# Scaling the rows of the later groups' scans three slots ahead of their step, and not two

## The chip, the cores and the metric

The kernel runs on one core of one Trainium2 chip. The metric is the time of the kernel on the device in microseconds. The median of three runs of the kernel before is 3759.6 us (3755.57 to 3771.47).

## What is computed

The input x has 32 sequences of 256 tokens with 256 features. The result is `x + ffn(cond(x))`, all in fp32. Cut to what matters here:

```python
def cond(x, t_emb, ...):
    xr, gate = split(x @ W_in.T, 2)            # 512 inner features each
    xc = silu(causal_conv(xr + t_emb, 4 taps))
    xn = layernorm(xc)
    B, C, dt = split(xn @ W_xproj.T, 3)        # 16 states each
    ad = 1 - 0.01 * tanh(dt @ W_dt.T + b_dt) * tanh(A_log)
    bd = B * min(norm(xn), 1)
    for t in range(256):                       # the scan
        h = clip(h * ad[t] + bd[t] * xn[t], -10, 10)   # h: 32 x 16 x 512
        y[t] = sum over the 16 states of C[t] * h
    return (y + D * xn) * silu(gate) @ W_out.T

def ffn(x):                                    # two layers
    x = x + local_attention(shift(x))          # 8 heads of 64, window 128
    x = x + (a * gelu(g)) @ w2                 # a, g from layernorm(shift(x)) @ w1
```

The scan is serial in its 256 tokens. Attention and feed-forward of a sequence need the scan's output for that sequence, and nothing of other sequences.

## The kernel before

**Tiling of the scan.** The 32 sequences are cut into four groups (NG) of eight (GB). For a group the state h is one tile of 128 partitions (16 states of 8 sequences) by 512 inner features. The 256 steps of a group are cut into eight chunks of 32 (CH). The kernel divides the state by the running product of the decays, so that the decay leaves the loop: within a step there remains `h = clamp(h + xrep, +-lim)`, where xrep is the token's row of xn, times a factor beta for each partition. Four functions carry one step:

- `load_rows` (L672): SyncE (SP) issues a DMA that reads the token's row of xn from DRAM and spreads it over the 128 partitions. It moves 256 KB into a tile of the pool xp, which has six buffers (L225). The tile is called xrep.
- `scale_row` (L689 to L698): ScalarE (ACT) multiplies the tile by beta, in place (the instruction is that of L693).
- `step` (L700 to L707): VectorE (DVE) makes the new h with one custom instruction (L703). The pool hp has eight buffers of h. With it the xrep buffer comes free, so the load of row n+6 can start when step n has ended.
- `read_out` (L710 to L721): four 32-column matmuls on TensorE (PE) multiply four states h by C. They free the buffers of h.

**What a chunk needs beforehand.** The input is projected (L395) and convolved: `conv_in` on GpSimd (acc, L474), `conv_taps` on VectorE (acc, L485), `conv_th` on ScalarE (th, L493), `conv_out` on VectorE (xc, L498). Then it is normalised (st, mv, ve, stat, xn; L547 to L566) and written to DRAM as xnd. Out of it come the chunk's figures: `figures_in` (bcd, L614), `decay_th` (ad, a tanh on ScalarE, L628) and `decays` (L633 to L647), in which VectorE finishes beta (L641). No row of the chunk can be scaled before that.

**Order by slots.** The work of a scan is put into slots. `at(s, function, ...)` puts a call into slot s, and in the slot of step t of a chunk that starts at s0 the calls are: the step of row t; the load of row t+6; the scale of row t+2. Beta is due in slot s0-5, and `read_out` of four rows five slots after the first of them. Each slot has two parts: the agenda with the step is traced first, the one with loads and scales after it.

**Order by stages.** Group 0's scan runs alone (`alone` is true for it), and a part of its rows is spread by TensorE and not by a DMA (`by_tensor`). Afterwards the scan of the next group runs beside attention and feed-forward of the group before it. These are cut into stages, eight for each sequence and layer, 128 for each group. After each stage `scan_to` advances the scans by a number of slots, two on average (L1466 on). So the calls of both are traced interleaved. After the third group's attention no scan is left, and the last group's attention and feed-forward run by themselves.

**What the builder does.** Out of the traced calls the builder makes each engine's queue of instructions. It takes the traced order as priority, but puts an instruction further ahead or behind by when it reckons it to be ready. A few calls are held, among them the scales of the later groups: `tc.keep_in_program_order(scaled)` (L698) keeps each behind what was traced before it on ScalarE. Scales of different rows may still change places: rows 0, 2, 4, 14 and 30 of a chunk are scaled three to five rows ahead of an earlier row in nearly every chunk.

**Attention and feed-forward** beside it, with the names that the trace uses: ps_qkv (L962), the matmuls of the projection to q, k and v; sq (ACT, L975), rot, swp and ss (DVE and POOL, L978 to L995), which normalise and rotate q and k; qT and kT (ACT, L1006), which take the turned q and k out of PSUM; sc, pT and v_sb (L1143 to L1177), the scores and their exponentials; oT (ACT, L1213; DVE, L1230), the attention's output; rinv (DVE, L1195); hn and hT, the normalised input of the feed-forward; pa (PE, L1301) and ag (ACT, L1309; DVE, L1317), its widening matmuls and the gated product; po_f and fo (L1329, L1340), the narrowing. All matmul results share one tag of PSUM with eight banks (L229).

Of the kernel before, what the change touches and what calls it, by code (L numbers as in the profile page):

```python
# [73 lines left out]
def kernel(  # L74
# [139 lines left out]
    for i in range(2):  # L214
        t = const.tile([P, NI * (P + GB)], FP, tag=f"ly{i}", name=f"ly{i}")
# [3 lines left out]
    def program(ctx, exact):  # L219
# [153 lines left out]
        def group_scan(g):  # L373
# [8 lines left out]
            alone = g == 0  # L382
# [5 lines left out]
            def at(s, what, *args):  # L388
                agendas[-1].setdefault(s, []).append(partial(what, *args))
# [276 lines left out]
            def by_tensor(t):  # L666
                return alone and t % (2 * NQ) < XR
# [171 lines left out]
            for c in range(NCH):  # L839
                s0 = c * CH  # L840
# [35 lines left out]
            for c in range(NCH):  # L876
                s0 = c * CH
                at(s0 - 43 if alone else s0 + 6, load_x, c)
                if alone:
                    for ch in range(NC_):  # L880
                        at(s0 - 40 + 2 * ch, project, c, ch)
                else:
                    for i in range(2):
                        at(s0 - 44 + 2 * i, load_projected, c, i)
                for ch, s in enumerate((13, 16, 17, 18)):
                    at(s0 + s, project, c, NC_ + ch)
                at(s0 - 27, raw_sums, c)
                for j in range(NJ):
                    at(s0 - 26 + 4 * j, norm_turn, c, j)
                at(s0 - 8, figures_out, c)  # L890
                for t in range(CH):
                    if not by_tensor(t):
                        at(s0 + t - 6, load_rows, c, t)
                    if by_tensor(t) and t % XR == 0:
                        at(s0 + t - 4, spread_rows, c, t)
                    at(s0 + t - 2, scale_row, c, t)
                for hb in range(CH // TB):
                    s = s0 + hb * TB
                    at(s - 9 if alone else s + 7, load_skip, c, hb)
                    at(s + 23, out_turn, c)  # L900
                for d in range(KM):
                    at(s0 + 43 + 2 * d, project_y, c, d)
# [11 lines left out]
        def scan_slots(groups):  # L914


            slots, scans = {}, [group_scan(g) for g in groups]
            for part in range(2):
                for i, agendas in enumerate(scans):
                    for s, what in agendas[part].items():  # L920
                        slots.setdefault(i * S + s, []).extend(what)
            for s in range(min(slots), max(slots) + 1):
                for what in slots.get(s, ()):
                    what()
                yield s
# [531 lines left out]
        s0 = done[0]  # L1457
# [130 lines left out]
```

## Time and profile before

| | |
|---|---|
| median of three runs | 3759.6 us |
| the profiled execution's own time | 3750.83 us |
| its span, first to last instruction | 3748.7 us, granted clock 0.987 |
| group 0's scan alone | 0 to about 460 us |
| scans of groups 1 to 3 beside attention and feed-forward | about 460 to 2910 us |
| last group's attention and feed-forward alone | 2910 to 3749 us |
| one chunk of 32 steps in the joint phase | about 108 us, 3.4 us for each slot |
| step (DVE L703) | 1024 instructions, 926 ns on average |
| scale (ACT L693) | 960 instructions, 719 ns on average |
| load of a row (256 KB) | 960, 3.3 to 4.0 us from issue to landing |

The profile is one execution. A group of instructions is given by line, engine, operation and tiles (out<-in), then its count, its busy time in us, the mean of one in ns, and the engine's idle time just before such instructions with what ended most of it. In the timeline each line has its start in us, its duration in us, the engine and the line, and in square brackets the idle time before it and what released it. In a list of waits the three numbers are the sum of the waits in us, their number and the longest. In the table of stretches each pair is an engine's busy time and its number of instructions, in the order PE, PEld (weight loads), DVE, ACT, POOL, and after them the granted clock, the share of the DMA engines and GB/s.

### The profile page before, as it was taken

How to read it: one execution, taken by the hardware profiler on the slowest of the kernel's cores; microseconds unless marked ns; L12 is line 12 of the kernel's file. 1: busy time of each engine (PE TensorE's matmuls, PEld its weight loads, DVE VectorE, ACT ScalarE, POOL GpSimd, SP SyncE). 2: the span in 40 equal slices, each digit the busy share in tenths (PEclk: the TensorE clock that was granted, in tenths of full speed). 3: DMA queues.
4: the chain of work that ended last, by engine and by line, in shares of the span. 5: the costliest groups of instructions: out<-in, count | busy, mean ns of one | idle time of the engine just before them, and what ended most of it. 6: DMA issues, size and time to landing. Idle time of an engine off the chain costs nothing.

```text
span 3748.7 us, 57254 instructions
## 1 busy us (share of the span) xinstructions
PE 3601.1 (96%) x19900; PEld 2242.4 (60%) x19900; DVE 2669.6 (71%) x5177; ACT 2195.4 (59%) x3817; POOL 1834.9 (49%) x1776
## 2 busy tenths in 40 slices
PE   7999889999999999999999999999999999999998
PEld 4444335656656665665666665656666666666666
DVE  6888889888787787778777877777777444444443
ACT  4666656666666666666666665666666444444442
POOL 4433466545555565455455555645444444434441
PEclk9999999999999999999999999999999999999999
DMA  7777655445454545434444545444443211011101
GB/s 210 205 198 202 189 163 149 120 117 135 127 137 129 147 123 146 120 112 122 120 128 116 147 124 147 121 108 126 112 129 103 57 40 50 12 34 34 30 25 35
DMA packets 469214, 435.81 MB, mean 116 GB/s; under 512 B 228835, under 2 KB 308532, under 8 KB 468788
## 3 DMA queue, kind: packets, MB, share of 16 engines
q1 hardware_dynamic: 384466, 420.05, 40.1%
q10 hardware_dynamic: 84450, 12.01, 2.0%
q8 instruction: 160, 2.62, 0.3%
q14 instruction: 138, 1.13, 0.1%
HBM read 383.70 MB, written 46.66 MB: 115 GB/s over the span
## 4 chain that ended last, share of the span: by engine, by line
PE 62%; DVE 16%; POOL 7%; ACT 6%; DMA 5%; issue 3%; SPq 0%; ACTq 0%; DVEq 0%; POOLq 0%
PE ps_qkv L962 12%; PE pa L1301 12%; PE po_f L1329 7%; DVE h L703 6%; PE y L715 4%; PE ps_wo L1012 4%; DMA xrep<-xnd 4%; PE sc L1168 4%; PE ov L1206 3%; PE ps_out L793 2%; ACT xrep L693 2%; DVE acc L485 2%; PE tr_qk L1001 2%; PE ps_in L395 2%; POOL acc L474 2%
## 5 line engine op out<-in xcount | busy, mean ns | idle before, releaser
L703 DVE CUSTOM_DVE_ANT_0 h<-h,xrep,lim 128x512 f32<-128x512 f32 x1024 | 948.2, 926 | 269.2 <-ACT xrep L693 238.8
L693 ACT ACTIVATE xrep<-xrep,beta 128x512 f32<-128x512 f32 x960 | 674.1, 719 | 333.0 <-DMA xrep<-xnd 235.9
L962 PE MATMUL ps_qkv<-qkv,res 128*128 128x512 f32 x1536 | 727.1, 610 | 45.2 <-DVE ag L1317 30.1
L1301 PE MATMUL pa<-hT,w 128*128 128x256 f32 (+1 forms) x3072 | 688.3, 386 | 0.3 <-ACT oT L1213 0.3
L1301 PEld LDWEIGHTS pa<-hT,w 128*128 128x128 f32 (+1 forms) x3072 | 492.9, 178 | 183.7 <-issue 66.5
L962 PEld LDWEIGHTS ps_qkv<-qkv,res 128*128 128x128 f32 x1536 | 282.4, 194 | 335.4 <-issue 263.3
L986 POOL TENSOR_TENSOR rot<-rot,swp 128x512 f32<-128x512 f32 x256 | 336.5, 1314 | 293.0 <-DVE swp L983 239.2
L1258 POOL TENSOR_TENSOR rstd<-ve,neg_half 128x1 f32<-128x1 f32 x128 | 82.7, 646 | 792.9 <-DVE ve L1256 787.8
L994 POOL TENSOR_TENSOR rn<-ss,neg_half 128x8 f32<-128x8 f32 x256 | 460.3, 1798 | 14.8 <-DVE ss L992 5.0
L1329 PE MATMUL po_f<-ag,w 128*128 128x256 f32 (+1 forms) x1536 | 387.8, 394 | 4.8 <-DVE res L1340 1.1
L715 PE MATMUL y<-h,ly 128*32 128x512 f32 x2048 | 354.9, 612 | 12.9 <-DVE h L703 11.7
L1329 PEld LDWEIGHTS po_f<-ag,w 128*128 128x128 f32 (+1 forms) x1536 | 273.6, 190 | 112.9 <-issue 44.6
L1317 DVE SCALAR_TENSOR_TENSOR ag<-pa,b_sb,ag 128x256 f32<-128x256 f32 (+1 forms) x448 | 212.4, 474 | 166.5 <-ACT ag L1309 163.0
L975 ACT ACTIVATE sq<-ps_qkv 128x512 f32<-128x512 f32 x256 | 152.1, 596 | 270.5 <-PE ps_qkv L962 234.6
L995 POOL TENSOR_TENSOR rot<-rot,rn 128x512 f32<-128x512 f32 x256 | 298.6, 1166 | 20.1
L1309 ACT ACTIVATE ag<-pa,b_sb 128x256 f32<-128x256 f32 x320 | 150.4, 470 | 198.5 <-PE pa L1301 197.4
L1012 PE MATMUL ps_wo<-oT,wo 128*128 128x256 f32 x1024 | 231.6, 379 | 0.0
L485 DVE SCALAR_TENSOR_TENSOR acc<-xr,wc_sb,acc 128x256 f32<-128x256 f32 x384 | 192.7, 525 | 52.9 <-POOL acc L474 52.6
L1177 ACT ACTIVATE pT<-sc 128x512 f32<-128x512 f32 x384 | 208.5, 596 | 32.2 <-PE sc L1168 30.7
L1168 PE MATMUL sc<-qT,kT 64*128 64x128 f32 (+1 forms) x2048 | 221.5, 345 | 0.0
L978 DVE TENSOR_TENSOR rot<-ps_qkv,rc_sb 128x512 f32<-128x512 f32 x256 | 175.0, 683 | 56.5 <-ACT sq L975 55.9
L1012 PEld LDWEIGHTS ps_wo<-oT,wo 128*128 128x128 f32 x1024 | 194.5, 190 | 27.2 <-PE y L715 0.8
(150 smaller groups left out, 5534.7 us busy)
## 6 DMA issues: line engine op xcount, KB each, us to landing
xrep<-xnd SPq DMA_DIRECT2D x960, 256.0 KB
rb<-inv SPq DMA_DIRECT2D x128, 256.0 KB
xnd<-xn SPq DMA_DIRECT2D x64, 256.0 KB
qkv<-in_wqkv_dram SPq DMA_DIRECT2D x24, 512.0 KB
ahead<-xs_a SPq DMA_DIRECT2D x48, 256.0 KB
xp<-ahead SPq DMA_DIRECT2D x48, 256.0 KB
xd<-xnd SPq DMA_DIRECT2D x192, 64.0 KB
w<-in_w_dram SPq DMA_DIRECT2D x80, 128.0 KB
```

What stands on the lines that cost most here:

```text
L485: nc.vector.scalar_tensor_tensor(acc, xr[:, :, k : k + CH], wc_sb[:, ch, k : k + 1], acc, ALU.mult, ALU.add,)
L693: scaled = nc.scalar.activation(bx, ck[c].pop(("bx", t), bx), AF.Copy, scale=ck[c]["beta"][:, t : t + 1])
L703: nc.vector._custom_dve(TENSOR_ADD_SAT, out=h_new, in0=state["h"], in1=bx, s0=ck[c]["lim"][:, 0, t : t + 1], s1=ck[c]["lim"][:, 1, t : t + 1],
L715: nc.tensor.matmul(ck[c]["y", hb][32 * q : 32 * q + 32, :], ly[hb % 2][:, 32 * t : 32 * t + 32], ck[c].pop(("h", hb * TB + t)), start=(i = ...
L962: nc.tensor.matmul(ps, res[b][:, k, t0 : t0 + W], wt["qkv", a][:, k], start=(k == 0), stop=(k == KM - 1),)
L986: nc.gpsimd.tensor_add(rot, rot, swp)
L994: nc.gpsimd.tensor_tensor(rn, ss, neg_half, ALU.pow)
L995: nc.gpsimd.tensor_mul(rot, rot, bc(rn, 2, DH))
L1012: nc.tensor.matmul(po[:, d], wt["wo", 0][:, c, d * P : (d + 1) * P], oT[:, c, :], start=(c == 0), stop=(c == NC_ - 1),)
L1168: nc.tensor.matmul(banks[r][:, i, :], kT[rows, i0 + i, kw * W : (kw + 1) * W], qT[rows, i0 + i, kw * W :], start=False, stop=(i == n - 1),)
L1301: nc.tensor.matmul(pg if x else pa, wt["w1", m][:, k, x], self.h[:, k], start=(k == 0), stop=(k == KM - 1),)
L1329: nc.tensor.matmul(self.po[:, d], wt["w2", 0][r0 : r0 + n, m, d * P : (d + 1) * P], self.ag[m][r0 : r0 + n], start=(m == 0), stop=(m == le ...
```

## The change

One line of `group_scan` is changed. The scale of row t of a later group (`alone` is false) is put three slots ahead of step t, and not two. For group 0 it stays two slots. Load, step and read-out stay in their slots, and so do the buffers and what the functions do. In the slot of step t the scale that is called is now that of row t+3; its place behind the previous ACT instruction is held as before.

```diff
                     if not by_tensor(t):
                         at(s0 + t - 6, load_rows, c, t)
                     if by_tensor(t) and t % XR == 0:
                         at(s0 + t - 4, spread_rows, c, t)
-                    at(s0 + t - 2, scale_row, c, t)
+                    at(s0 + t - 2 if alone else s0 + t - 3, scale_row, c, t)
```

## The prediction

> **What bounds the kernel now.** I read the busy shares first, then the chain that ended last, the costliest groups, the busy time of three stretches, the waits of a steady stretch, and the timeline of one chunk.
>
> ```profile
> PE 3601.1 (96%) x19900; PEld 2242.4 (60%) x19900; DVE 2669.6 (71%) x5177; ACT 2195.4 (59%) x3817; POOL 1834.9 (49%) x1776
> ...
> PE 62%; DVE 16%; POOL 7%; ACT 6%; DMA 5%; issue 3%; SPq 0%; ACTq 0%; DVEq 0%; POOLq 0%
> ...
> L703 DVE CUSTOM_DVE_ANT_0 h<-h,xrep,lim 128x512 f32<-128x512 f32 x1024 | 948.2, 926 | 269.2 <-ACT xrep L693 238.8
> L693 ACT ACTIVATE xrep<-xrep,beta 128x512 f32<-128x512 f32 x960 | 674.1, 719 | 333.0 <-DMA xrep<-xnd 235.9
> ```
>
> TensorE is the bound: the scan can only cost time where it keeps TensorE waiting. Steps wait 238.8 us for scaled rows and scales wait 235.9 us for loads, which looks like the prize of an earlier scale; the next views show how little of it TensorE feels.
>
> ```profile
> 0.00:460.00 460.00, 407.20 (x1689) 207.54 (x1690) 376.12 (x719) 269.07 (x495) 186.12 (x266) 0.95 0.74 201
> 2000.00:2500.00 500.00, 480.94 (x2759) 302.80 (x2755) 386.90 (x746) 311.13 (x547) 268.13 (x257) 0.99 0.46 127
> 2910.00:3749.00 839.00, 827.89 (x4722) 559.31 (x4719) 362.82 (x783) 380.88 (x623) 333.96 (x278) 1.00 0.13 35
> ```
>
> The columns are the stretch in us, its length, and busy time of PE, PEld, DVE, ACT and POOL. In the first stretch group 0 scans alone, and in the last nothing scans; the change touches neither. Between lies the joint phase, some 2450 us. In its steady part TensorE is idle 500 − 480.94 = 19.1 us in 500. By its gaps it is idle 26.8 us in 430 to 645 and 59 us in 645 to 2700: no change of the scan's order can win more than these.
>
> ```profile
> DVE h L703 <- ACT xrep L693: 61.1, 32, 3.6
> ...
> PE ps_qkv L962 <- DVE ag L1317: 10.4, 5, 2.7
> ```
>
> These are waits between 2000 and 2500 (sum, number, longest). The steps wait 61.1 us; TensorE's one regular stall, 10.4 us in 5 waits, is about one per chunk of 32 steps. Over the joint phase there are 13 such stalls, from 1310.79 to 2606.19, 108 us apart, 30.1 us in sum. The timeline shows how one comes about:
>
> ```profile
> 2139.33 0.48 DVE L485 SCALAR_TENSOR_TENSOR acc<-xr,wc_sb,acc 128x256 f32<-128x256 f32 x1 [0.93 <-POOL acc L474]
> ...
> 2142.11 2.01 POOL L474 TENSOR_SCALAR acc<-xr,wc_sb,bconv_sb 128x256 f32<-128x256 f32 x1 [2.66 <-DVE xc L498]
> ...
> 2160.71 0.72 ACT L693 ACTIVATE xrep<-xrep,beta 128x512 f32<-128x512 f32 x1 [2.75 <-DVE beta L641]
> ...
> 2168.33 0.72 ACT L693 ACTIVATE xrep<-xrep,beta 128x512 f32<-128x512 f32 x1 [3.56 <-DMA xrep<-xnd]
> 2170.18 0.81 DVE L703 CUSTOM_DVE_ANT_0 h<-h,xrep,lim 128x512 f32<-128x512 f32 x1 [3.42 <-ACT xrep L693]
> ...
> 2172.75 4.31 PE L962 MATMUL ps_qkv<-qkv,res 128*128 128x512 f32 x6 [2.58 <-DVE ag L1317]
> ```
>
> At each chunk's start the first row's scale stands at the head of ACT's queue until VectorE has beta. Then a row scaled out of turn (804, five rows ahead) waits 3.56 us for its load, since that load was issued only when step 798 freed a buffer at 2164.70. Rows 799 and 800 queue behind it, VectorE waits 3.42 us, and the ag behind step 800 reaches TensorE 2.58 us late.
>
> **What the Trainium skill says.** "PSUM — Partial Sum Buffer", section "Engine vs sequencer instructions", has the queues of ScalarE, VectorE and GpSimd as strict FIFO. The trace agrees: behind the scale of 804 the copy of oT stands, its matmul done at 2162.6, and it starts at 2168.96. "SBUF — State Buffer", section "Who interferes with whom", says that a VectorE instruction with two SBUF inputs and a GpSimd instruction that reads SBUF exclude each other. A step has two such inputs, h and xrep: it takes 0.81 us in most places and 1.84 at 2157.97, beside GpSimd's products; the mean is 0.926. A step that moves can pay or save up to 1.0 us. "Perfetto Trace Analysis", section "Optimization Strategy", tells to find the engine's gaps and what blocks it; the 13 equal gaps are where I price the change.
>
> **The change, part by part.** It takes nothing away and adds nothing: 768 scales of 0.72 us on ACT are called one slot earlier, after a different ACT instruction, to which their order is then held. The rest is traced as before, but the builder orders each engine anew. I read the order of both programs as built, engine by engine, and set it against the times of the trace.
>
> ACT: 616 of the 768 scales move, by 3.4 instructions on average. Each place that held row t holds row t+1. The rows scaled far ahead of their turn remain: before, rows 0, 2, 4, 14 and 30 of a steady chunk go 3 to 5 rows ahead; after, rows 1, 3, 5, 15 and 31. So the waits for loads remain as well, shifted by a row: a row five ahead still needs the buffer of the step just before it (six buffers). Row 1 takes the place where row 0 waits for beta, and row 0's scale, which needs beta too, stands before it: the same wait. Cost of this part: nothing.
>
> SP: 250 of 768 row loads move two places up. A load leaves 0.03 us after the step six rows earlier has ended and lands 3.3 to 4.0 us later; its moment is set by the step and not by SP. Other loads on SP's queue lose at most that wait, and none of the 13 stalls ends on one. Nothing.
>
> VectorE: 511 of 768 steps move up, by 4.9 positions, mostly one step in the place of its forerunner. Rows 12 to 18 of a chunk stay, where the y matmuls, four rows at a time, must free h buffers (eight). TensorE: 131 of 11,553 instructions move, so its demand is the same. GpSimd: 330 of 1759, following.
>
> What is then different on the chain to the stall? In the chunk of the timeline two steps (792 and 793) come ahead of two xc instructions and an acc that waits 0.93 us for GpSimd. Their scales can end by 2139.2; the second step takes 0.81 after that and ends at 2140.05, and the second xc can begin near 2140.5 in place of 2141.52: 1.0 us earlier. GpSimd's acc, which waited 2.66 us for xc, starts 1.0 us earlier, and with it the acc and rot ahead of beta. One more acc (0.48) leaves this stretch and returns ahead of beta, net nothing; between rot and beta four steps stand before and after. So beta comes about 1.0 us earlier, the links after it are the same, and the stall of 2.58 shrinks to 1.6. Its bounds: 0, where the acc waits elsewhere; and 2.5 to 3.0, if the steps in between also meet less of GpSimd.
>
> Against it: in this chunk the tanh of conv (th) goes behind two scales and is 1.5 to 2.2 us later; the conv's xc for it is 2.4 us later (2137.65 to 2140.05), but GpSimd needs its result only 1.8 later, within its own 2.66 wait. That cover is part of the sum above; without it 0.6 us is lost.
>
> Rows 14 and 15 are the risky place. Before, the order is scale 810, a table load, ag, sq, xn, scales 813 and 814; after, scale 811, xn, scales 814 and 815, then table load and ag. Row 815's load needs step 809. The trace has step 808 from 2190.05 to 2190.86; if step 809 follows it directly, it ends at 2191.7, the row lands 3.5 later at 2195.2, the scale ends at 2195.9, the table load (1.28) at 2197.2. The ag ran at 2195.99, so it is 1.2 us late; but the sq behind it waited for TensorE until 2197.77, and the ag after it has until 2201.6. So nothing reaches TensorE.
>
> Sum: 13 steady chunks × 1.0 = 13 us less. The chunks of 460 to 1290 don't repeat, and I add nothing for them, ±10. Against the profiled execution (3750.83, span 3748.7 and 2.1 around it) that gives 3737.8; the median of the runs is 8.8 higher, 3759.6, and so 3746.6, say 3747.
>
> **The rivals.** *Full gain:* beta comes 2.5 to 3 us earlier and the 13 stalls go. For: the wait is one serial chain and each link is short. Against: the beta, load and scale links are unchanged in number. It gives −30 us (the 30.1 of the waits), 3730; with the small stalls beside them (0.8 for scores and 0.9 for rinv in every other chunk, 11 us) 3719. What is late next is then TensorE itself.
>
> *Nothing changes:* the one-row shift leaves every wait in its place, and the freed microsecond goes back to the next row's load. For: the out-of-turn rows are the same pattern. It gives 3760 ± 5. That the edit doesn't do what it says is ruled out by the 616 moved scales.
>
> *Slower:* ACT stands at its queue's head for a row that hasn't landed, with TensorE's evacuations behind it. Place: row 15 ahead of the table load and ag, and rows 1 to 5 likewise. With step 809 at its old end, 2192.69, the row lands at 2196.2, the scale ends at 2196.9 and the table load at 2198.2: ag is 2.2 us late and the sq behind it 0.9. Eight banks hold all matmul results, so once both are late, TensorE waits. It decides when step 9 of a chunk ends later than about 1 us after its new place. If two such places a chunk pass on 1.5 us each, 14 chunks give 42 us: 3802. For: 235.9 us of ACT's idle time are such waits already, and the steps of rows 12 to 18 don't move up with their scales. Against: only one of the pairs stands directly before an evacuation without slack.
>
> **How the numbers follow.** About 0.5% (18.8 us) is what a measurement of this kernel can tell from no change. Small gain 0.40 (3747, its own range 3736 to 3758), nothing 0.12, full gain 0.18, slower 0.30. Faster by over 0.5% is below 3740.8: the full gain less a little, and a fifth of the small gain, 0.17 + 0.07 = 0.24. Slower is above 3778.4: 0.28 of the 0.30. The same: 0.48. The range runs from the full gain's lower end, 3719, to the slower case's 3802, which leaves out about 0.15 above and 0.03 below.
>
> **What would show it.** Right: the 13 stalls of ps_qkv on ag near 1.6 us each, the sum of the waits 560 to 2910 near 17 and not 30.1; beta about 1 us nearer to rot; steps' wait for scales near 239 us; the stretch of 839 us after the last step unchanged. Wrong: new TensorE stalls on ag or sq near rows 14 to 16 of a chunk, with an ACT wait for xrep's load just ahead of them (the slower rival); no such stalls left at all (full gain); or a gain or loss in the chunks before 1290, for which my sum has no term.

## The result and the profile after

| | before | after |
|---|---|---|
| median | 3759.94 us (20 runs) | 3768.05 us (20 runs) |
| ratio, 95% interval | | 1.0024, 1.0014 to 1.0033 |
| span of the profiled execution, granted clock | 3748.7 us, 0.987 | 3763.8 us, 0.986 |

Three slots are 8 us slower. The forecast was 13 us faster: wrong in its sign, though both changes are within half a per cent. The two profiled executions differ by 15.1 us, of which 6.1 us are there already when group 0's last step starts (459.9 and 466.0 us), in a part that the change doesn't touch; so single stretches of two profiles are compared below, and the whole by the ratio.

The page of the kernel after, with the shares and the steps of the scan:

```profile
PE 3597.9 (96%) x19900; PEld 2240.2 (60%) x19900; DVE 2682.6 (71%) x5177; ACT 2196.7 (58%) x3817; POOL 1824.0 (48%) x1776
...
L703 DVE CUSTOM_DVE_ANT_0 h<-h,xrep,lim 128x512 f32<-128x512 f32 x1024 | 942.0, 920 | 192.3 <-ACT xrep L693 109.0
```

The work is the same and TensorE is the bound as before. VectorE's wait for scaled rows fell from 238.8 to 109.0 us, which is what an earlier scale is for, and the kernel is slower. The lists of waits from 560 to 2910 us, before and then after, show where VectorE waits instead: at ag, 91.9 us where it was 33.5, and at y's matmuls, for a free buffer of h, 21.0 where it was 4.2.

```profile
ACT xrep L693 <- DMA xrep<-xnd: 135.0, 66, 6.5
...
DVE ag L1317 <- ACT ag L1309: 33.5, 48, 2.5
...
DVE h L703 <- PE y L715: 4.2, 13, 1.9
```

```profile
ACT xrep L693 <- DMA xrep<-xnd: 154.2, 83, 5.7
...
DVE ag L1317 <- ACT ag L1309: 91.9, 63, 6.0
...
DVE h L703 <- PE y L715: 21.0, 13, 1.9
```

TensorE's idle time is the length of a stretch less the time in which TensorE is busy. The stretches run between the same qT copies in both traces:

| TensorE idle, us | before | after |
|---|---|---|
| first chunks (510 to 1352 us before) | 34.4 | 45.4 |
| steady chunks (1352 to 2647 us before) | 42.3 | 47.1 |

The runs below add traces with two and with three slots in a stretch, and the two kinds don't overlap: 34.2 to 38.5 us against 43.7 to 47.4 in the first chunks, 42.3 twice against 45.2 to 47.1 in the steady ones. But the table shows where TensorE waits, and not how much time is lost. The idle time rises by 15.8 us and the time by 8. The steady stretch even became shorter, 1295.6 us before and 1292.2 after, since TensorE was busy for 1253.3 us before and 1245.2 after, at a granted clock of 0.99 and 1.00. The first chunks became longer, 842.0 and 854.3 us.

TensorE's waits from 1310 to 2700 us, before and then after, show how the steady part changed:

```profile
PE ps_qkv L962 <- DVE ag L1317: 30.1, 13, 2.7
PE ps_qkv L962 <- DVE rinv L1195: 6.3, 12, 0.9
...
PE ov L1206 <- DVE ag L1317: 1.1, 6, 0.3
```

```profile
PE ps_qkv L962 <- DVE ag L1317: 19.8, 11, 2.4
PE ps_qkv L962 <- DVE rinv L1195: 11.4, 13, 0.9
PE ov L1206 <- DVE ag L1317: 10.0, 12, 1.1
PE tr_qk L1001 <- DVE ag L1317: 6.0, 7, 1.8
```

The stalls that the prediction priced fell by 10.3 us, and the gap at sc by 2.7 (from 4.9). Waits at ov, tr_qk and rinv rose by 8.9, 6.0 and 5.1.

**A steady chunk.** It is the chunk of the prediction's timeline. First TensorE's other gaps there before (the prediction shows the one of 2.58), then all of them after, then ScalarE after:

```profile
2147.61 0.38 PE L1161 MATMUL sc<-mask_t,ident_b 128*128 128x512 bf16 x1 [0.81 <-DVE ag L1317]
2161.07 1.52 PE L1206 MATMUL ov<-pT,v_sb 128*64 128x256 f32 x16 [0.15 <-DVE ag L1317]
2166.81 1.98 PE L962 MATMUL ps_qkv<-qkv,res 128*128 128x512 f32 x4 [0.21 <-DVE rinv L1195]
```

```profile
2163.92 0.38 PE L1161 MATMUL sc<-mask_t,ident_b 128*128 128x512 bf16 x1 [0.30 <-DVE ag L1317]
2178.35 1.52 PE L1206 MATMUL ov<-pT,v_sb 128*64 128x256 f32 x16 [1.11 <-DVE ag L1317]
2185.08 1.99 PE L962 MATMUL ps_qkv<-qkv,res 128*128 128x512 f32 x4 [0.94 <-DVE rinv L1195]
2190.01 2.41 PE L962 MATMUL ps_qkv<-qkv,res 128*128 128x512 f32 x5 [1.58 <-DVE ag L1317]
```

```profile
2177.99 0.72 ACT L693 ACTIVATE xrep<-xrep,beta 128x512 f32<-128x512 f32 x1 [3.85 <-DVE beta L641]
2178.61 0.57 ACT L1006 COPY qT<-tr_qk 128x512 f32<-128x512 f32 x1
```

The stall of 2.58 us at ps_qkv is 1.58, the size forecast. But ov, ahead of it, now waits 1.11 us and not 0.15 for an ag that stands behind beta on VectorE, and rinv costs 0.94 and not 0.21. (Before, rinv's wait was short in every other steady chunk; now it is 0.63 or more in all.) Before, the chunk had 0.81 + 0.15 + 0.21 + 2.58 = 3.75 us of gaps; now 0.30 + 1.11 + 0.94 + 1.58 = 3.93. From the start of that ov to ps_qkv it is 11.68 us before and 11.66 after: this part of the chain is no shorter, and the stall at its end is smaller only because TensorE comes to it later. VectorE shows why ov waits, before and then after:

```profile
2147.48 0.67 DVE L978 TENSOR_TENSOR rot<-ps_qkv,rc_sb 128x512 f32<-128x512 f32 x1
...
2160.54 0.48 DVE L1317 SCALAR_TENSOR_TENSOR ag<-pa,b_sb,ag 128x256 f32<-128x256 f32 x1
```

```profile
2163.78 0.68 DVE L978 TENSOR_TENSOR rot<-ps_qkv,rc_sb 128x512 f32<-128x512 f32 x1
...
2172.89 1.26 DVE L485 SCALAR_TENSOR_TENSOR acc<-xr,wc_sb,acc 128x256 f32<-128x256 f32 x1
2174.18 1.39 DVE L468 TENSOR_TENSOR xr<-xp,cond_sb 128x256 f32<-128x256 f32 x1
...
2177.82 0.48 DVE L1317 SCALAR_TENSOR_TENSOR ag<-pa,b_sb,ag 128x256 f32<-128x256 f32 x1
```

From rot to that ag it was 2147.48 to 2160.54, 13.06 us; now it is 2163.78 to 2177.82, 14.04. The acc that the steps displaced landed beside GpSimd's products (L995, L745), takes 1.26 us and not 0.48, and the xr behind it takes 1.39 and not 0.41. Before, a step and a small instruction stood there and took longer in the same way (1.84 for 0.81, 1.02 for 0.23). Set against the twelve matmuls of po_f that start at 2135.57 before and at 2152.37 after, GpSimd's acc (L474) comes 1.0 us earlier, as forecast, the ag ahead of rot 0.5 earlier, and beta 0.5 later.

**A first chunk.** ScalarE of the kernel after near 825 us:

```profile
827.24 0.72 ACT L693 ACTIVATE xrep<-xrep,beta 128x512 f32<-128x512 f32 x1 [2.25 <-DMA xrep<-xnd]
827.87 1.05 ACT L1213 COPY oT<-ov 128x512 f32<-128x512 f32 x2
```

Row 388 waits 4.53 us for its load, row 390 then the 2.25 shown, and both oT copies wait behind row 390. TensorE's waits from 560 to 1310 us, before (one line) and then after:

```profile
PE ps_qkv L962 <- ACT oT L1213: 1.8, 2, 1.3
```

```profile
PE ps_qkv L962 <- ACT oT L1213: 7.1, 3, 2.9
...
PE ov L1206 <- DVE res L1020: 4.8, 1, 4.8
...
PE ov L1206 <- DVE ag L1317: 3.5, 2, 2.2
```

Before, the wait of ov for res wasn't there. In the three waits for oT, ACT stands just ahead of the copy at rows 390, 479 and 513, whose loads haven't landed.

### The profile page after: what moved, and what is told of

It reads as the page before. It is cut to its first block, busy times and chain, and to the rows that moved or that the text cites. A ratio compares the mean times of both kernels' runs of the same rounds, so it can differ in the third digit from the quotient of the medians.

```text
span 3763.8 us, 57292 instructions
## 1 busy us (share of the span) xinstructions
PE 3597.9 (96%) x19900; PEld 2240.2 (60%) x19900; DVE 2682.6 (71%) x5177; ACT 2196.7 (58%) x3817; POOL 1824.0 (48%) x1776
## 4 chain that ended last, share of the span: by engine, by line
PE 65%; DVE 18%; DMA 6%; POOL 4%; issue 4%; ACT 3%; SPq 0%; ACTq 0%; DVEq 0%; POOLq 0%
PE ps_qkv L962 13%; PE pa L1301 12%; PE po_f L1329 8%; DVE h L703 6%; DMA xrep<-xnd 5%; PE y L715 4%; PE sc L1168 4%; PE ps_wo L1012 4%; PE ov L1206 3%; PE ps_in L395 3%; DVE acc L485 2%; PE ps_out L793 2%; PE tr_qk L1001 2%; PE rs L1187 2%; PE sc L1161 2%
## 5 line engine op out<-in xcount | busy, mean ns | idle before, releaser
L703 DVE CUSTOM_DVE_ANT_0 h<-h,xrep,lim 128x512 f32<-128x512 f32 x1024 | 942.0, 920 | 192.3 <-ACT xrep L693 109.0
L962 PE MATMUL ps_qkv<-qkv,res 128*128 128x512 f32 x1536 | 716.8, 603 | 43.0 <-DVE ag L1317 21.0
L1329 PEld LDWEIGHTS po_f<-ag,w 128*128 128x128 f32 (+1 forms) x1536 | 274.6, 190 | 117.1 <-issue 45.4
L995 POOL TENSOR_TENSOR rot<-rot,rn 128x512 f32<-128x512 f32 x256 | 294.4, 1150 | 20.1
L485 DVE SCALAR_TENSOR_TENSOR acc<-xr,wc_sb,acc 128x256 f32<-128x256 f32 x384 | 202.8, 554 | 49.9 <-POOL acc L474 49.5
```

Source lines behind the costliest of these rows:

```text
L485: nc.vector.scalar_tensor_tensor(acc, xr[:, :, k : k + CH], wc_sb[:, ch, k : k + 1], acc, ALU.mult, ALU.add,)
L703: nc.vector._custom_dve(TENSOR_ADD_SAT, out=h_new, in0=state["h"], in1=bx, s0=ck[c]["lim"][:, 0, t : t + 1], s1=ck[c]["lim"][:, 1, t : t + 1],
L962: nc.tensor.matmul(ps, res[b][:, k, t0 : t0 + W], wt["qkv", a][:, k], start=(k == 0), stop=(k == KM - 1),)
L995: nc.gpsimd.tensor_mul(rot, rot, bc(rn, 2, DH))
L1329: nc.tensor.matmul(self.po[:, d], wt["w2", 0][r0 : r0 + n, m, d * P : (d + 1) * P], self.ag[m][r0 : r0 + n], start=(m == 0), stop=(m == le ...
```

## The experiments

All ratios are to the kernel before, run on the same chip. Idle times are those of one trace for each run, between the same qT copies as above. The scale's slot is the line of the change; `first` stands for `g == 1 or (g == 2 and c == 0)`, rows 256 to 543.

**Which chunks.**

```diff
-at(s0 + t - 2, scale_row, c, t)
+at(s0 + t - 3 if first else s0 + t - 2, scale_row, c, t)                         # first chunks
+at(s0 + t - 3 if g == 3 or (g == 2 and c > 0) else s0 + t - 2, scale_row, c, t)  # later chunks
```

> Rows scaled three slots ahead only in the eight chunks of group 1 and the first chunk of group 2 (rows 256 to 543, about 460 to 1310 us), two slots elsewhere. My theory: the whole loss is made in these first chunks of the joint phase, where scales held by their loads stand before the attention's oT copies on ACT; ratio to before 1.002 to 1.004 (8 to 15 us longer), and TensorE's waits for oT copies of 2 us and more between 800 and 1220 are there as in the changed kernel. Rival: the loss is spread over all chunks in proportion, then about 9 of 24 chunks carry it, ratio 1.0009. Rival: the loss is group 0's or the steady chunks', ratio 1.000.

Measured 1.0012 (1.0001 to 1.0023); TensorE idle 43.7 us in the first chunks, and 42.3 in the steady ones, as before.

> The complement: three slots ahead only from the second chunk of group 2 on (rows 544 to 1023), two before. My theory: these chunks are neutral, since what they gain ahead of rot (0.5 us a chunk) they give back between rot and beta; ratio 0.999 to 1.001, and the pattern of stalls of a steady chunk is that of the changed kernel (ov on ag near 1.1 us, ps_qkv on ag near 1.6). Rival (spread loss): 1.0015. Rival (my forecast): 0.9965, 13 us shorter.

Measured 1.0009 (1.0001 to 1.0017); 38.5 us idle in the first chunks and 45.8 in the steady. The two add to 1.0021, about the whole. Each part is clear of 1 by very little, and the split is open: by the ratios it is about half and half, with intervals from nearly nothing to nearly all; by the idle time the first chunks carry more. So that they carry all of it isn't borne out. Much of the scatter goes with the granted clock: the 43 executions of the kernel before that these two runs are set against go from 3744 us at 0.990 to 3767 us at 0.981. A straight line through these and the runs' own (about 2.3 us for 0.001, an estimate) leaves 4.5 us for the first chunks and 6.9 for the later ones at equal clock, each ±2. So both parts are there.

**More and fewer slots**, `t - 4` and `t - 1` for all later groups.

> Four slots ahead for all later groups. If scales that wait for their loads at the head of ACT's queue cost the time, one slot more makes more of it: ACT's wait for loads in 560 to 2910 rises above the 154 us of three slots, ratio to before 1.004 to 1.010. If the first chunks' loss is only an accident of one order, four slots can fall on either side of three: 0.998 to 1.004.

Measured 1.0040 (1.0026 to 1.0054), with 55.1 us idle in the steady chunks. ACT's wait for loads rose to 185.9 us, as expected; but the interval reaches into the rival's range.

> One slot ahead for all later groups. If earlier scales hold ACT's queue, one slot holds it less: ACT's wait for loads falls below the 135 us of two slots; but VectorE's steps then wait longer for scales (225 us at two slots, 96 at three), and what is queued behind them on VectorE: ratio 1.000 to 1.010. If the time is monotone in the slots through ACT's waits alone, 0.998.

Measured 0.9999 (0.9989 to 1.0010). But the trace is not that of before: 42.7 us idle in the first chunks (34.4 before) and 29.7 in the steady (42.3). Two effects seem to cancel. ACT's wait for loads didn't fall: 135.1 us.

> Two slots in the first chunks (rows 256 to 543) as before, one slot in all later chunks. One slot everywhere left the time as it was, but its trace has TensorE idle 8 us more in the first chunks and 1.0 to 1.4 us less in each of 12 later ones. My theory: both parts are real and separable, so this keeps the gain alone: ratio 0.996 to 0.9975, TensorE's idle time in 645 to 2700 about 12 us less than before. Rival: the profile's small gaps are no measure of time; ratio 1.000.

```diff
-at(s0 + t - 2, scale_row, c, t)
+at(s0 + t - 2 if alone or first else s0 + t - 1, scale_row, c, t)
```

Measured 0.9935 (0.9921 to 0.9949), better than expected: the effects are separable. The steady chunks were idle for 28.1 us, 14.2 less; the time fell by more than that.

**Without the loads.** The output lacks the later groups' rows.

```diff
 def load_rows(c, t):
     xr = xp.tile([P, DI], FP, tag="xrep", name="xrep")
     ck[c]["rep", t] = xr
+    if not alone:
+        return
...
-        bx, ck[c].pop(("bx", t), bx), AF.Copy, scale=ck[c]["beta"][:, t : t + 1]
+        bx, ck[c].pop(("bx", t), bx) if alone else dskip_sb, AF.Copy, scale=ck[c]["beta"][:, t : t + 1]
```

> Leaves out the row loads of the later groups: a scale there reads a resident tile and writes a free xrep buffer, so ACT waits for the buffer (the step six rows earlier) and no longer for a transfer. Two slots ahead. My theory: ACT's 135 us of waits for loads cost TensorE little with two slots, ratio to before 0.996 to 1.000. It is the partner of the next run.

Measured 0.9830 (0.9817 to 0.9844), outside what I expected: the loads' waits stood behind most of the steady idle time, 42.3 us before and 6.1 here. The steady stretch is 53 us shorter, though, of which 36 are idle time; the other 17 are the same matmuls, which took 1236.2 us and not 1253.3, at a granted clock of 1.00 and not 0.99.

> The same without loads, with three slots ahead. My theory: what three slots lose in the first chunks is the wait of scales for their loads, with oT copies behind; without loads three slots are no slower than two: within 0.1% of the run without loads at two slots, and TensorE's 2 us waits for oT copies between 800 and 1220 are gone. Rival: the loss comes from VectorE's order (acc and steps standing in a different order), which the loads don't touch: three slots stay 0.2% slower than two.

Measured 0.9857 (0.9840 to 0.9873), 3698.5 against 3691.2 us for the partner: three slots lose 0.2% without loads too. My theory fell, and the rival's number came true. TensorE's waits from 1310 to 2700 us, two slots and then three, both without loads (two lines longer, so ov and ag stand two lines lower):

```profile
PE ov L1208 <- DVE ag L1319: 0.9, 6, 0.2
```

```profile
PE ov L1208 <- DVE ag L1319: 11.0, 12, 1.1
```

One wait per chunk is new, and it is ov's for the ag behind beta: the stall of the steady chunk above, with no load in it. In the first chunks the waits of ps_qkv for oT are gone, as my theory had it; but 34.2 us are idle against 27.8: of the 11 us that three slots cost there with loads, 6.4 stay. In the steady chunks the idle time is 14.0 us against 6.1.

**Steps.** What if VectorE's order stayed as it is? Each step of the later groups is held behind what was traced before it:

```diff
-nc.vector._custom_dve(
+stepped = nc.vector._custom_dve(
...
+if not alone:
+    tc.keep_in_program_order(stepped)
```

> Scales two slots ahead; besides, each step of the later groups is held behind what was traced before it on VectorE, as the scales are on ACT. In a steady chunk acc and xr then stand ahead of rot, and three steps between rot's part and beta. It is the partner of the next run. If VectorE's work between rot and beta sets the stall, it may be faster than before by itself: ratio 0.993 to 1.003.

Measured 1.0613 (1.0598 to 1.0627), far off: the steps come so late that TensorE waits 186.5 us at y for h in 560 to 2910, where it waited 0.9 us before.

> The same with three slots. With the steps held, VectorE's order is nearly that of the partner (277 of 5165 instructions differ, against over 500 steps between the two kernels of the study), TensorE's is the same; only the scales on ACT stand one slot earlier. Theory now, after the runs without loads: about half of the loss, and all of it in steady chunks, comes from VectorE's order. So three slots against two here lose at most 0.1%, and no stall of ov on ag that the partner lacks. Rival: the scales' places on ACT alone cost the time: 0.2 to 0.3% slower than the partner.

Measured 1.0819 (1.0804 to 1.0834), 1.9% above the partner, and far outside both cases. The waits from 560 to 2910 us, two slots and then three:

```profile
ACT xrep L693 <- DMA xrep<-xnd: 104.9, 73, 5.1
```

```profile
ACT xrep L693 <- DMA xrep<-xnd: 416.6, 196, 8.8
```

That is the price of an earlier scale with the steps held: a load leaves when the step six rows before it has ended, so if the steps don't come earlier, the scale stands longer at the head of ACT's queue. In the kernel of the study the steps were moved as well, and ACT's wait rose by 19 us only.

> The steps held, with two slots in the first chunks and one in the later. If the two gains add, it is the fastest of all: below the 0.9935 of the run with two slots, then one. If holding the steps loses what the free order won, it lies between 0.9935 and 1.002.

Measured 1.0621 (1.0606 to 1.0635): nothing to add to a loss of 6%, and outside both cases that I gave.

**The displaced acc.**

```diff
+e = int(ch == 0 and not (alone or first))
-at(s0 - 38 + 2 * ch, conv_in, c, ch)
+at(s0 - 38 + 2 * ch - e, conv_in, c, ch)
```

and so for conv_taps, conv_th and conv_out, with three slots in the later chunks.

> As the run with three slots in the later chunks only, and there the convolution of channel block 0 (conv_in to conv_out) called one slot earlier, which puts the acc that had fallen between rot and beta ahead of rot again, with one more step between rot and beta in its place. My theory: that acc (1.26 us there, beside GpSimd) and the xr behind it (1.39 for 0.41) are what gave the gain back; so 0.5 to 1.4 us less TensorE idle time per chunk than in that run: ratio to before 0.996 to 0.9995. Rival: the step that takes their place costs the same, nothing changes: 1.001.

Measured 1.0009 (1.0000 to 1.0018), the same as without the edit, and 45.8 us idle in the steady chunks, again the same: the rival. In the trace acc stands ahead of rot again and xr takes 0.41, but the step in acc's place takes 1.53 and the small instruction behind it 1.25 for 0.23. From rot to the ag behind beta it is 14.21 us, no shorter than with acc there.

The other way to put acc back is to hold one step. With three slots, for `g == 1 and c == 1 and t == 25`, and then for `not alone and t == 25`:

> Three slots, and one single step (row 313, row 25 of group 1's second chunk) held behind what was traced before it on VectorE, so that it stands behind xc and acc again. In the trace of three slots it stood ahead of xc, GpSimd's acc came late, VectorE waited 3.20 us for it with res behind, and TensorE's ov waited 4.80 us for res. Theory (VectorE's order makes the loss in the first chunks that the loads don't): that stall of 4.80 us near 604 is gone, and TensorE's idle time up to 700 falls by 3 to 5 us against three slots; the time by about 0.1%, ratio to before 1.0005 to 1.002. Rival (the stall comes from elsewhere and only shows there): the stall stays.

Measured 1.0029 (1.0020 to 1.0039). The stall stays: ov waits 5.69 us for res, and the theory about that stall falls. VectorE there:

```profile
594.15 0.48 DVE L485 SCALAR_TENSOR_TENSOR acc<-xr,wc_sb,acc 128x256 f32<-128x256 f32 x1 [5.43 <-POOL acc L474]
```

VectorE stands at acc for GpSimd, and res runs behind it at 595.73. With the step ahead of xc, in the kernel of the study, it waited 3.20 us at the same acc, so moving that step back doesn't help.

> Three slots, and the step of row 25 held so in every later chunk. In a steady chunk acc and xr stand ahead of rot again, as with two slots, with step 793 in their place behind it. Theory (acc and xr between rot and beta gave back the gain): ov's wait of 1.1 us a chunk shrinks to 0.3 or less, the 1.0 us won before rot may be lost; TensorE's idle time per steady chunk falls by 0.3 to 1.0 us: ratio to before 0.997 to 1.001. Rival: the step in their place costs the same, ratio 1.002 as with three slots.

Measured 1.0037 (1.0026 to 1.0049). From TensorE's gaps in the steady chunk:

```profile
2175.31 1.52 PE L1208 MATMUL ov<-pT,v_sb 128*64 128x256 f32 x16 [0.47 <-DVE ag L1319]
...
2187.31 4.97 PE L964 MATMUL ps_qkv<-qkv,res 128*128 128x512 f32 x7 [2.76 <-DVE ag L1319]
```

Acc and xr stand ahead of rot, a fifth step stands behind it, and from rot to the ag behind beta it is 13.38 us in place of 14.04. ov's wait falls from 1.11 to 0.47. But sc has its 0.82 back and ps_qkv its 2.76: what is taken from one stall of the chunk goes to the next. Its sum, with rinv's 0.36, is 4.41 and no smaller, and the steady chunks are idle for 47.1 us, as with three slots alone. So no order with three slots that was tried gives the loss back, and the place of acc and xr explains where the wait lies, not the whole loss. In the first chunks ps_qkv's waits for oT fell here from 7.1 to 2.8 us, and the idle time stayed at 46.6.

**The wait for beta.** One slot had won in the later chunks. In its trace the scale of the chunk's first row stands behind the copies of qT and kT. So only row 0 is moved, in the later chunks and then in all chunks of groups 1 to 3:

```diff
-at(s0 + t - 2, scale_row, c, t)
+at(s0 + t - 2 + (t == 0 and not (alone or first)), scale_row, c, t)
+at(s0 + t - 2 + (t == 0 and not alone), scale_row, c, t)
```

> As before, two slots, but row 0 of each later chunk (from row 544 on) one slot ahead, which puts its scale, the one that waits for beta, behind the copies of qT, kT and v_sb that it held. What made one slot faster in the later chunks: if it is this wait for beta, most of the 26 us are here as well, ratio 0.993 to 0.996; if it is the sum of all rows' places, 0.998 to 1.002.

Measured 0.9910 (0.9895 to 0.9925), 3718.3 us, more than one slot for all rows gave. ScalarE in the chunk of the timeline:

```profile
2143.97 0.58 ACT L1006 COPY qT<-tr_qk 128x512 f32<-128x512 f32 x1
...
2144.91 0.74 ACT L693 ACTIVATE xrep<-xrep,beta 128x512 f32<-128x512 f32 x1
```

Nothing waits for beta ahead of qT any more (2.75 us before, 3.85 with three slots), row 797 follows, and the step behind it frees the next load. The stalls of ps_qkv for ag fall from 30.1 us to 1.5, and the steady idle time from 42.3 to 18.9. The steady stretch is 33 us shorter, 23 of them idle time; again the rest is busy time, at a granted clock of 1.00.

> Two slots, and row 0 at one slot in every chunk of groups 1 to 3, also in the first ones. If the wait for beta costs in the first chunks as in the later, 0.5 to 1% faster than row 0 in the later chunks alone, ratio to before 0.988; if the first chunks' order is only good with what it was planned for, as with one slot everywhere, slower than that: 0.991 to 0.995.

Measured 0.9893 (0.9876 to 0.9909), 3717.3 us, between the two cases that I gave. Its interval overlaps with that of the run before it, so the two aren't told apart. The first chunks were idle for 35.9 us, no less than before (34.4), so no gain from moving row 0 shows there. These two are the fastest versions of the study that compute everything.

## Why the prediction was wrong

- *TensorE is the bound, and only its gaps count.* Right: VectorE's wait for scales more than halved, and the time rose.
- *The places shift by a row and the waits with them.* Right for the loads: ACT's wait for them rose by 19 us only (135.0 to 154.2), since steps and loads came along; the pair with held steps shows what it costs if they don't. That the steps' wait for scales would stay near 239 us was wrong (109.0): I had the steps move with the scales, and part of VectorE's waiting moved to ag and to the buffers of h. Nor does row 0's scale stand ahead of row 1's: row 801 waits for beta with 3.85 us, where row 800 waited 2.75, and row 800 is scaled at 2186.63, after it.
- *"One more acc (0.48) leaves this stretch and returns ahead of beta, net nothing ... So beta comes about 1.0 us earlier."* This is the step that failed for the steady chunks. GpSimd's acc did come 1.0 us earlier. But from rot to the ag behind beta it took 0.98 us more, and beta came 0.5 later against the same matmuls. Beside GpSimd the acc and the xr behind it cost 2.65 us where I had 0.48 and 0.41; other instructions met less of GpSimd in turn. The price stood in the prediction, as a step that takes 1.84 for 0.81, but I didn't use it for the acc.
- *"The stall of 2.58 shrinks to 1.6."* The number came true in this chunk (1.58), by luck: not because beta was earlier, but because TensorE had waited at ov and rinv already. Summed over 560 to 2910 the stalls were 21.0 us and not 17, with 6.0 more at tr_qk, for the ag ahead of rinv. I priced one gap, and not the sum of the gaps on the chain. I had 13 times 1.0 us less; the idle time of the steady chunks rose by 4.8.
- *"The chunks of 460 to 1290 don't repeat, and I add nothing for them, ±10."* The second step that failed, a term put at nothing only because it was hard to work out: TensorE's idle time rose by 11.0 us there. The run with three slots in these chunks alone was 0.12% slower (0.01 to 0.23), so they carry a part of the loss, about half or less.
- *The slower rival* had a mechanism that is there, in the wrong place: scales whose rows haven't landed hold evacuations behind them, not at rows 14 and 15 of steady chunks, where no such stall appeared, but at rows 390, 479 and 513 of the first chunks, with oT behind (7.1 us in three waits, 1.8 before). Without loads these are gone. It isn't the main cause: a loss of 0.2% stays without loads, and in the run with row 25's steps held these waits shrank and the time didn't.
- *The full gain*, the end of these stalls, was there to be had, but by moving the scale that waits for beta later, not the others earlier.

What stays open: first, the part of the first chunks' loss that remains without loads, 6.4 us of idle time. It lies on VectorE by its waits (ov for res and ag), but holding the step that I took for its cause didn't remove it. Second, the steady chunks. That the place of acc and xr makes most of ov's longer wait is shown by the run that put them back (0.47 for 1.11). That GpSimd's products made them long is argued from the trace, and no run with three slots brought the idle time back to 42.3 us. Third, how much of the 0.24% each of the two parts carries.

## What to carry to other kernels

An earlier call on an in-order queue can be worth nothing if what it waits for doesn't come earlier too. Ask what starts the transfer: if that is a step of the same loop, as here, the call merely stands longer at the head of the queue. Price all gaps of the bounding engine along a chain together, since here a gap that closed handed its time to the next one. And look for the one instruction whose operand is latest, here row 0's scale behind beta: moving that one out of the way of the rest, one slot later in each chunk, won 0.9 to 1.1%, while moving all rows earlier lost 0.24%.

## What was not expected of the hardware

Leaving out the row loads made the kernel 1.7% faster although the DMA engines were busy for only 46% of the time in the steady part. That points to the 3.3 to 4.0 us from a step to its row, and not to the bandwidth, but no run separates the two.

Where TensorE idled much less, the granted clock of the steady stretch was higher, and the time fell by more than the idle time did. The clock was 0.95 and 0.96 with 176 and 135 us of idle time (steps held, three slots and two), 0.99 with 42 (before), and 1.00 with 19 (row 0 at one slot) and 6 (no loads). It isn't strict: the kernel after has 1.00 with 47. Whether the shorter gaps raise the clock was not tested.
